# Distances on GpSimd in place of comparisons on VectorE, in the first stage of a two-layer graph-attention kernel

## The chip, the cores and the metric

One core of a Trainium2 chip runs the whole program. The metric is the device time of one execution in microseconds (us); lower is better. The median of three runs of the kernel before is 651.15 us (650.93 to 651.38). A difference of 0.2%, 1.3 us, is about what a measurement of this kernel can tell from none.

## The reference

The kernel computes two graph-attention layers on 512 nodes with 768 features, then a residual and a layer norm. There are 16896 edges (`src`, `dst`), sorted by `dst`.

```
def gat_layer(x, W, a_s, a_d, b, edge_index, concat):
    h = (x @ W).reshape(n, H, C)              # H = 8 heads of 768, then 1 head of 768
    alpha_s = einsum('nhc,hc->nh', h, a_s)
    alpha_d = einsum('nhc,hc->nh', h, a_d)
    e = leaky_relu(alpha_s[src] + alpha_d[dst], 0.2)
    e = exp(e - segment_max(e, dst)[dst])
    alpha = e / (segment_sum(e, dst)[dst] + 1e-16)
    return segment_sum(h[src] * alpha[:, :, None], dst) + b

h = elu(gat_layer(x, W1, a_src1, a_dst1, b1, ...))
out = layernorm(x + gat_layer(h, W2, a_src2, a_dst2, b2, ...))
```

The kernel replaces the edge list by a dense 512 x 512 table `cnt` (how often node s is a source of node d) and works with dense attention from there on. Building that table is the part that the change touches.

## The kernel before

**The stages.** The first stage, some 62 us, builds `cnt` and at the same time computes the first head's features `HS[0] = x @ W1[0]`. After it comes a loop over the 8 heads (attention, aggregation, the second layer's matmul, the next head's features), and at the end the second layer's attention and the layer norm. The loop and the end are the same in both kernels.

**Counting.** The edges lie as 132 chunks of 128 edges, one edge per partition. For a chunk `c`, a count is a matmul of two tables that are made from the indices:

- `os`, 128 x 512: which of the 512 nodes is the edge's source. `one_hot` (L512) makes it on VectorE by a comparison (`is_equal`, L517) or, for the 128 destinations of group `S = 2`, on ScalarE as a step function (`Sign`, L515), which `counted_by_steps` (L399) turns back into counts by a difference of neighbours. `os` tiles come from a ring of 32 buffers.
- `od` (profile name `odw`), 128 x 210 x 32: which of 32 neighbouring destination nodes is the edge's destination. Since the edges are sorted, each chunk can only hit one or two blocks of 32 nodes; there are 210 (chunk, block) pairs. `destinations(lo, hi)` (L491) makes a quarter of `od` in one VectorE instruction (L493), 128 x 1632 or 128 x 1728 elements: `rel` (destination minus the block's base) compared with 0 to 31.

`count` (L532) issues the matmuls of a batch (L543); a matmul takes the 32 columns of `od` as weights, and four blocks of 32 rows go side by side. When all of a group's blocks are done, ScalarE and VectorE move the group from PSUM into `cnt` and `absent`.

**The order** of everything is written out by hand (a manual schedule): what the Python program emits first, an engine runs first. The loop over `batches` (L575) has nine rounds. A round emits: the quarter of `od` if one of its chunks is the first of a new quarter (quarter 0 in round 0, quarter 2 in round 1, quarter 1 in round 3, quarter 3 in round 5); `sources`, the VectorE `os` of the round, with the pending `empty` steps of matmul results in the middle; `extra` steps such as `weight_sums`, the Strassen-like sums of `x` (`s1` to `s4`) or logits; then some products of the first projection, `items[pos]`, each followed by its `empty` (a ScalarE copy `hs`, L426, or a VectorE add, L428) and by some ScalarE `os` of the next round (`ahead`, `share` of them per product); then `count`.

- The products come in the order P1, P2, P5, P3, P6, P7, P4, two halves each, six matmul instructions of 128x384 per half (L305). They go through PSUM buffers `held` (2) and `mm` (3).
- `turn_x(t, r)` (L200) transposes a piece of `x` on TensorE into an `mm` buffer, and ScalarE copies it to `xT` (L205). Pieces (0,1), (1,1) follow product 1, pieces (2,0), (3,0), (2,1), (3,1) follow product 3.
- `found` and `pst` (L614) add up the edges that lie in their blocks; if not all do, a general pass follows. With these inputs it does not.

**The weights.** The sums of W1 that the products need are partly made by accumulating DMAs on GpSimd's queue: `additions0[0]` (L160) adds W1 parts into `t2` (for P6), L381 into the part for P7, `additions0[1]` (L161) from `t2` into `t4` (for P4). GpSimd writes such a DMA's descriptors itself. `load_w1(1)` and its sums (L106, L117, L160, L161 again) follow on the same queue. `weight_sums` emits all of them. The DMAs from SyncE's and ScalarE's queues count on a ring of eight semaphores, so a DMA is issued only when the eighth one before it has landed.

Of the kernel before, what the change touches and what calls it, by code (L numbers as in the profile page):

```python
# [8 lines left out]
F32 = mybir.dt.float32  # L9
F16 = mybir.dt.float16  # L10
BF16 = mybir.dt.bfloat16
I32 = mybir.dt.int32
U16 = mybir.dt.uint16
AF = mybir.ActivationFunctionType
ALU = mybir.AluOpType
# [21 lines left out]
def gat_pass(  # L37
# [16 lines left out]
    nc = tc.nc  # L54
    P = 128
    N, D = x.shape
    H = a_src1.shape[0]
    E = src.shape[0]
    NT = N // P
    DC = D // P  # L60
    HALF = D // 2
    EC = E // P
    EH = EC // 2
    HK = DC // 2
    HN = N // 2
    L, R = slice(0, HALF), slice(HALF, D)
# [10 lines left out]
    ohp = counting.enter_context(tc.tile_pool(name="onehot", bufs=1))  # L77
# [20 lines left out]
    W1, W2, A = {}, {}, {}  # L98
# [22 lines left out]
    def load_w1(h, slot="w2"):  # L121
        return load_w(W1, h, slot, w1[:, h * D:(h + 1) * D])
# [15 lines left out]
    def block(m, r, cols):  # L138
        return m[r * HK * P:(r + 1) * HK * P, cols].rearrange("(k p) d -> p k d", p=P)

    w1_0 = w1[:, :D]
    for r, cols in enumerate((L, R)):
        nc.scalar.dma_start(x_sb[:, :2, cols], x[:2 * P, cols].rearrange("(t p) d -> p t d", p=P))
        nc.sync.dma_start(W1[0][r][:, :, L], block(w1_0, r, L))
    for t in (2, 3):
        nc.sync.dma_start(x_sb[:, t, :], x[t * P:(t + 1) * P, :])
    b1_rows = ohp.tile([H * DC, P], F32, name="b1_rows")
# [5 lines left out]
    def sums_by_dma(W_, m, slot):  # L153

        lo_, hi_, t1_ = W_
        t2, t4 = (wpool.tile([P, HK, HALF], F32, name=f"{slot}t{j}") for j in (2, 4))
        for t_, cols in ((t2, R), (t4, L)):
            nc.sync.dma_start(t_, block(m, 1, cols))

        additions = [lambda: nc.gpsimd.dma_start(t2, t1_, accum_op=ALU.add),  # L160
                     lambda: nc.gpsimd.dma_start(t4, t2, accum_op=ALU.add)]  # L161
        return dict(P1=lo_[:, :, L], P2=hi_[:, :, L], P3=hi_[:, :, R], P4=t4, P5=t1_, P6=t2,
                    P7=lo_[:, :, R]), additions
# [16 lines left out]
    nodes = ohp.tile([P, N], F16, name="nodes")  # L180
# [6 lines left out]
    ones = const.tile([P, 1], F32, name="ones")  # L187
# [3 lines left out]
    for j in range(2):  # L191
        nc.vector.tensor_reduce(picks[:, j:j + 1], ident.rearrange("p (j k) -> p k j", k=32)[:, j, :], axis=AX.X,
                                op=ALU.add)
# [6 lines left out]
    def turn_x(t, r):  # L200

        ps = mm.tile([P, 512], F32, name="mm")
        for k in range(HK):
            nc.tensor.transpose(ps[:, k * P:(k + 1) * P], x_sb[:, t, (r * HK + k) * P:(r * HK + k + 1) * P], ident)
        nc.scalar.copy(xT[:, r * HK:(r + 1) * HK, t * P:(t + 1) * P],  # L205
                       ps[:, :HALF].rearrange("p (k n) -> p k n", n=P))
# [4 lines left out]
    if general:  # L211
        nc.vector.tensor_copy(idx_f, idx_i)
        idx = ohp.tile([P, 2, EC], F32, name="idx")
# [6 lines left out]
    else:  # L220
# [3 lines left out]
        B, SLACK = 32, 10  # L224
        blocks = []
        for c in range(EC):
            m = (c + 0.5) * P * N / E
            b = int(m // B)
            lo, hi = b - (m - b * B < SLACK), b + ((b + 1) * B - m < SLACK)
            blocks.append(range(max(lo, 0), min(hi, N // B - 1) + 1))  # L230
        at = [0]
        for b in blocks:
            at.append(at[-1] + len(b))
        NB = at[EC]
# [5 lines left out]
        lo = 0  # L240
        while lo < EC:
            hi, k = lo + 1, len(blocks[lo])
# [7 lines left out]
            lo = hi  # L250
# [9 lines left out]
        rel = ohp.tile([P, NB], F16, name="rel")  # L260
        nc.vector.tensor_tensor(rel, psi[:, :NB], base, op=ALU.subtract)
        idx = ohp.tile([P, EC], F32, name="idx")
# [55 lines left out]
    def logits(h, feats, t):  # L318
        for al, a, sign in zip(AL[h], A[h], (1.0, -1.0)):
            nc.vector.scalar_tensor_tensor(scr, feats[:, t, :], sign, a, op0=ALU.mult,  # L320
                                           op1=ALU.mult, accum_out=al[:, t:t + 1])
# [52 lines left out]
        ]  # L374
        return [pair(p, i, *rest) for p, *rest in steps for i in range(2)]

    def weight_sums():

        nc.vector.tensor_tensor(W1[0][2], W1[0][0][:, :, L], W1[0][0][:, :, R], op=ALU.add)
        additions0[0]()  # L380
        nc.gpsimd.dma_start(W1[0][0][:, :, R], block(w1_0, 1, R), accum_op=ALU.add)  # L381
        additions0[1]()
        load_w1(1, "w2")()
        B_, additions1 = sums_by_dma(W1[1], w1[:, D:2 * D], "w2")
        for f in additions1:
            f()
        return B_
# [67 lines left out]
    def leak(q):  # L455
        nc.vector.scalar_tensor_tensor(q, q, NEG_SLOPE, q, op0=ALU.mult, op1=ALU.min)
# [18 lines left out]
    if not general:  # L475


        S = 2
# [9 lines left out]
        cps, done = {}, set()  # L488
        od = ohp.tile([P, NB, B], BF16, name="odw", bufs=1)

        def destinations(lo, hi):  # L491
            lo, hi = at[lo], at[hi]
            nc.vector.tensor_tensor(od[:, lo:hi, :],  # L493
                                    rel[:, lo:hi].unsqueeze(2).to_broadcast([P, hi - lo, B]),
                                    nodes[:, :B].unsqueeze(1).to_broadcast([P, hi - lo, B]),
                                    op=ALU.is_equal)

        def inside():

# [2 lines left out]
            nc.vector.scalar_tensor_tensor(below, rel, 0.0, below, op0=ALU.is_ge, op1=ALU.mult, accum_out=found)  # L502

        nidx = ohp.tile([P, EC], F32, name="nidx")
        nc.scalar.activation(nidx, idx, AF.Copy, bias=0.5, scale=-1.0)

        def by_steps(b):
            return b * B // P == S
# [1 line left out]
        hot = {}  # L510

        def one_hot(c, steps):  # L512
            hot[c, steps] = o = ohp.tile([P, N], BF16, name="os", bufs=32)
            if steps:
                nc.scalar.activation(o, nodes, AF.Sign, bias=nidx[:, c:c + 1])  # L515
            else:
                nc.vector.tensor_scalar(o, nodes, idx[:, c:c + 1], None, op0=ALU.is_equal)  # L517
# [40 lines left out]
        s1, s2, s3, s4 = xsums  # L558

        def ask():  # L560
            nc.vector.tensor_scalar(flag, pst[:1, :1], -1.0, float(E), op0=ALU.mult, op1=ALU.add)

        extra = {0: [inside], 1: [lambda: B1.update(weight_sums()), ask, s1, s2, s4], 3: [s3],
                 5: [lambda: logits(0, HS[0], 0)],
                 6: [lambda: logits(0, HS[0], 1), lambda: logits(0, HS[0], 2)], 7: [lambda: logits(0, HS[0], 3)]}
        B1 = {}
        wants = [3, 4, 7, 10, 12, 14, 16, 18]
        batches = []
        for ours, theirs in ((16, 0), (8, 8), (8, 8), (12, 4), (12, 4), (12, 4), (13, 3), (14, 2), (4, 0)):
            take = [order[k][:m] for k, m in ((False, ours), (True, theirs))]  # L570
            del order[False][:ours], order[True][:theirs]
            batches.append(take[0][:ours // 2] + take[1] + take[0][ours // 2:])
        assert not any(order.values())
        pos, made, quarter, waiting = 0, set(), EC // NT, []
        for n, batch in enumerate(batches):  # L575
            for k in sorted({c // quarter for c in batch} - made):
                destinations(k * quarter, (k + 1) * quarter)
                made.add(k)
            sources(kinds(batch, False), waiting)
            ahead = kinds(batches[n + 1], True) if n + 1 < len(batches) else []  # L580
            items_here = max(wants[n] - pos if n < len(wants) else 0, 1)
            share = -(-len(ahead) // items_here)
            waiting = []
            for f in extra.pop(n, []):
                f()
            while n < len(wants) and pos < wants[n]:
                if pos == wholes:
                    pairs = projection(1, XA, B1)
                    items += [(m, e, False) for m, e in pairs[:4]]
                multiply, empty, on_vector = items[pos]  # L590
                multiply()
                if on_vector:
                    waiting.append(empty)
                else:
                    empty()
                pos += 1
                for t, r in turns.get(pos, []):
                    turn_x(t, r)
                for c in ahead[:share]:
                    one_hot(c, True)  # L600
                del ahead[:share]
            assert not ahead
            if n == 2:
                turn_b1()
            if n + 1 == len(batches):
                spread(0)
                q = [lift(0, t) for t in range(NT)]
                for t in range(NT - 1):
                    leak(q[t])
                for t in range(NT - 1):  # L610
                    rank(q[t], t)
            if n == 0:
                pst = mm.tile([P, 512], F32, name="mm")
                nc.tensor.matmul(pst[:1, :1], found, ones, start=True, stop=True)  # L614
            if n == 3:
                again = nc.values_load(flag[:1, :1], min_val=0, max_val=E)
            count(batch, n + 1 == len(batches))
        assert not extra and not waiting and pos == len(items) and len(done) == NT
    else:
        for t in range(NT):  # L620
            ps = mm.tile([P, 512], F32, name="mm")
            for c in range(EC):
                o1 = ohp.tile([P, P], BF16, name="od", bufs=4)
                o2 = ohp.tile([P, N], BF16, name="os", bufs=32)
                nc.vector.tensor_scalar(o1, nodes[:, t * P:(t + 1) * P], idx[:, 0, c:c + 1], None,
                                        op0=ALU.is_equal)
                nc.vector.tensor_scalar(o2, nodes, idx[:, 1, c:c + 1], None, op0=ALU.is_equal)
                nc.tensor.matmul(ps[:, :N], o1, o2, start=c == 0, stop=c == EC - 1)
            counted(t, ps)
            for r in range(2):  # L630
                turn_x(t, r)
        turn_b1()
        B1 = weight_sums()
# [449 lines left out]
```

## Time and profile before

| what | value |
|---|---|
| median of three runs | 651.15 us |
| the profiled execution's own time | 651.15 us |
| its span, first to last instruction | 649.4 us |
| around the span (launch, end) | 1.75 us |
| busy: PE / DVE / ACT / POOL | 637.7 / 520.4 / 276.7 / 47.2 us |
| granted TensorE clock | 0.998 |

All times in the text below are us from the span's start in the profiled execution. PE is TensorE's matmuls, PEld its weight loads, DVE is VectorE, ACT is ScalarE, POOL is GpSimd, SP is SyncE. A line such as `L517 DVE TENSOR_SCALAR os<-nodes,idx` names the line of the kernel, the engine, the operation, and the tiles written and read. The chain is the run of work that ended last, followed back from the last instruction to what released each step. A timeline line holds the start, the length, the engine, and in square brackets how long the engine was idle before it and what ended that.

### The profile page before, as it was taken

To read this page: it belongs to the slowest core of one execution; us is meant where nothing else is said; L and a number is where in the kernel's file an instruction comes from. 1 tells how busy PE (TensorE), PEld (TensorE's weight loads), DVE (VectorE), ACT (ScalarE), POOL (GpSimd) and SP (SyncE) were. 2 spreads that over 40 slices of the span, in tenths; PEclk is the share of its full clock that TensorE was granted. 3 is DMA by queue.
4 is the path that set the end of the run, shared out by engine and by line. 5 is a ranking of instruction groups with operands and counts; after the bars stand their busy time and mean duration, and the time that the engine had idled before them with its cause. 6 is when DMAs were issued, how large, how long until landed. Compare 5 with 4: busy or idle time off the path is not lost.

```text
span 649.4 us, 7212 instructions
## 1 busy us (share of the span) xinstructions
PE 637.7 (98%) x2383; PEld 404.2 (62%) x2383; DVE 520.4 (80%) x1141; ACT 276.7 (43%) x481; POOL 47.2 (7%) x90
## 2 busy tenths in 40 slices
PE   8999999999999999999999999999999999999995
PEld 4544586557755586557755586557755586645553
DVE  8989989978779777878779777878779777876875
ACT  6774744530736045430736045430736045243440
POOL 1310020011000010011000110011000010000000
PEclk9999999999999999999999999999999999999999
DMA  9993499196806792196705793196706892000122
GB/s 320 327 202 86 79 330 287 36 260 207 196 0 164 161 275 97 37 262 201 197 1 144 180 276 97 37 264 204 193 1 167 207 250 97 25 1 1 32 58 78
DMA packets 77644, 97.97 MB, mean 151 GB/s; under 512 B 37095, under 2 KB 60447, under 8 KB 77599
## 3 DMA queue, kind: packets, MB, share of 16 engines
q1 hardware_dynamic: 63934, 75.80, 37.0%
q0 software_dynamic: 12976, 20.65, 18.3%
q10 hardware_dynamic: 688, 0.98, 0.5%
q8 instruction: 21, 0.34, 0.2%
q14 instruction: 25, 0.20, 0.1%
HBM read 85.09 MB, written 1.57 MB: 133 GB/s over the span
## 4 chain that ended last, share of the span: by engine, by line
PE 96%; ACT 1%; DMA 1%; DVE 1%; issue 0%; SPq 0%
PE mm L305 64%; PE mm L764 20%; PE mm L710 3%; PE mm L1035 3%; PE held L305 2%; PE tr L543 1%; DMA w<-in_L_gnn_W_dram 1%; ACT os L515 1%; PE bc L446 0%; PE bc L543 0%; PE tr L963 0%; PE tr L679 0%; ACT xT L205 0%; DVE os L517 0%; PE bc L985 0%
## 5 line engine op out<-in xcount | busy, mean ns | idle before, releaser
L305 PE MATMUL mm<-w,gT 128*128 128x384 f32 x288 | 97.4, 487 | 0.0
L305 PE MATMUL mm<-w,xT 128*128 128x384 f32 x264 | 88.4, 488 | 0.0
L305 PEld LDWEIGHTS mm<-w,gT 128*128 128x128 f32 x288 | 53.9, 190 | 35.3 <-issue 1.6
L305 PEld LDWEIGHTS mm<-w,xT 128*128 128x128 f32 x264 | 49.8, 190 | 35.7 <-ACT os L515 0.8
L768 ACT COPY u<-mm 128x256 f32<-128x256 f32 x21 | 7.8, 372 | 142.0 <-PE mm L764 142.0
L463 ACT ACTIVATE q<-q,nmax 128x512 f32<-128x512 f32 x36 | 25.8, 721 | 89.8 <-DVE nmax L461 89.8
L764 PE MATMUL mm<-PT,hs 128*128 128x256 f32 x252 | 61.3, 379 | 0.0
L305 PE MATMUL mm<-w1t,gS 128*128 128x384 f32 x180 | 60.7, 486 | 0.0
L305 PE MATMUL mm<-w2t,xS 128*128 128x384 f32 x168 | 56.6, 487 | 0.0
L764 PEld LDWEIGHTS mm<-PT,hs 128*128 128x128 f32 x252 | 47.8, 190 | 8.4 <-issue 0.4
L363 DVE TENSOR_TENSOR h<-h,mm 128x384 f32<-128x384 f32 x72 | 39.6, 550 | 14.6 <-PE mm L305 14.0
L305 PEld LDWEIGHTS mm<-w1t,gS 128*128 128x128 f32 x180 | 34.1, 190 | 23.6
L305 PEld LDWEIGHTS mm<-w2t,xS 128*128 128x128 f32 x168 | 31.8, 190 | 22.4 <-ACT q L452 0.4
L687 ACT COPY nr<-q 128x1024 uint16<-128x1024 uint16 x32 | 33.4, 1043 | 23.3 <-DVE q L673 15.8
L764 PE MATMUL mm<-pS,gS 128*128 128x256 f32 x168 | 43.2, 380 | 0.0
L692 ACT COPY PT<-zr 128x1024 uint16<-128x1024 uint16 x32 | 37.1, 1160 | 2.0 <-DMA zr<-nr 2.0
L764 PEld LDWEIGHTS mm<-pS,gS 128*128 128x128 f32 x168 | 31.8, 190 | 4.7 <-DVE pS L737 0.4
L305 PE MATMUL mm<-w,gS 128*128 128x384 f32 x96 | 32.6, 486 | 0.0
L305 PE MATMUL mm<-w1t,gT 128*128 128x384 f32 x96 | 32.5, 487 | 0.0
L305 PE MATMUL mm<-w,xS 128*128 128x384 f32 x96 | 32.5, 487 | 0.0
L106 POOL DMA_DIRECT2D w1t<-in_L_gnn_W_dram x7 | 8.9, 1267 | 310.7 <-PE mm L305 96.5
L363 DVE TENSOR_TENSOR u<-u,mm 128x384 f32<-128x384 f32 x28 | 15.4, 552 | 19.0 <-PE mm L305 18.7
(187 smaller groups left out, 1083.3 us busy)
## 6 DMA issues: line engine op xcount, KB each, us to landing
w<-in_L_gnn_W_dram SPq DMA_DIRECT2D x90, 384.0 KB, 6.3
w<-in_L_gnn_W_dram POOLq DMA_DIRECT2D x16, 576.0 KB, 9.7
w2t<-in_L_gnn_W_dram SPq DMA_DIRECT2D x10, 576.0 KB, 4.9
w1t<-in_L_gnn_W_dram SPq DMA_DIRECT2D x9, 576.0 KB, 4.6
w2t<-in_L_gnn_W_dram POOLq DMA_DIRECT2D x8, 576.0 KB, 9.8
w1t<-in_L_gnn_W_dram POOLq DMA_DIRECT2D x7, 576.0 KB, 8.7
a_s<-in_L_gnn_a_src_dram SPq DMA_DIRECT2D x8, 384.0 KB, 3.8
a_d<-in_L_gnn_a_dst_dram SPq DMA_DIRECT2D x8, 384.0 KB, 4.2
```

What stands on the lines that cost most here:

```text
L106: nc.gpsimd.dma_start(t1, upper[:, :, R], accum_op=ALU.add)
L305: nc.tensor.matmul(ps[:, :HALF], A_[p][:, k, i * P:(i + 1) * P], B_[p][:, k, :], start=start and k == 0, stop=k == HK - 1, skip_group_chec ...
L363: nc.vector.tensor_tensor(a, a, ps, op=ALU.subtract if p == "P7" else ALU.add)
L463: nc.scalar.activation(q, q, AF.Exp, bias=nmax, scale=-1.0)
L515: nc.scalar.activation(o, nodes, AF.Sign, bias=nidx[:, c:c + 1])
L543: nc.tensor.matmul(cps[t][r:r + B, :N], od[:, at[c] + b - blocks[c][0], :], h_, start=todo[b] == hits[b], stop=todo[b] == 1, tile_position ...
L687: nc.scalar.copy(apart.rearrange("p (h n) -> p h n", h=2), q.bitcast(U16).rearrange("p (n h) -> p h n", h=2))
L692: nc.scalar.copy(PT.rearrange("p s n -> p (s n)").bitcast(U16).rearrange("p (s n h) -> p s n h", s=NT, h=2)[:, :, t * P:(t + 1) * P, :], p ...
L710: nc.tensor.matmul(ps[:, :N], HS[h][:, s, c * P:(c + 1) * P], PT[:, s, :], start=(s == 0), stop=(s == NT - 1))
L764: nc.tensor.matmul(bank[p][:, :HN], A_[p][:, k, c * P:(c + 1) * P], B_[p][:, k, :], start=over is None and k == 0, stop=k == 1, skip_group ...
L768: nc.scalar.copy(u, part("P1"))
L1035: nc.tensor.matmul(ps[:, :cols.stop - cols.start], PT[:, s, t * P:(t + 1) * P], h2[:, s, cols], start=(s == 2), stop=(s == 1))
```

## The change

Four things are changed, all in the first stage.

1. Quarter 0 of `od` is still made by VectorE's comparison. The other three quarters are made in three instructions each: GpSimd subtracts (`rel` minus 0..31, into a float32 tile `dist`), GpSimd multiplies `dist` by itself, and ScalarE takes `Relu(1 - dist)`, which is 1 at distance 0 and 0 elsewhere. The GpSimd work of quarters 2 and 1 is emitted at the start, behind the `base` memsets and ahead of the first accumulating DMA; that of quarter 3 inside `weight_sums`, behind L381 and ahead of `additions0[1]`. `dist` has two buffers. The ScalarE step of quarter 2 is emitted after product 2, those of quarters 1 and 3 at the ends of rounds 2 and 4.
2. The first part of W1 (128 x 3 x 384) is loaded by three DMAs in place of one, so two more DMAs are in the ring of semaphores.
3. The step `nidx` moves behind product 1 and its transposes, the first round's ScalarE `os` are dealt two per product in place of three, and the batches change: group S gets 5, 5, 3, 0 chunks in rounds 4 to 7 where it had 4, 4, 3, 2, so its count is complete one round earlier.
4. The `os` ring shrinks from 32 to 30 buffers.

The core of the diff:

```diff
-        nc.sync.dma_start(W1[0][r][:, :, L], block(w1_0, r, L))
+        for ks in (slice(0, 1), slice(1, 2), slice(2, HK)) if r == 0 else (slice(0, HK),):
+            nc.sync.dma_start(W1[0][r][:, ks, L], block(w1_0, r, L)[:, ks])
...
     nc.gpsimd.dma_start(W1[0][0][:, :, R], block(w1_0, 1, R), accum_op=ALU.add)
+    if between:
+        between()
     additions0[1]()
...
-        def destinations(lo, hi):
-            lo, hi = at[lo], at[hi]
-            nc.vector.tensor_tensor(od[:, lo:hi, :],
-                                    rel[:, lo:hi].unsqueeze(2).to_broadcast([P, hi - lo, B]),
-                                    nodes[:, :B].unsqueeze(1).to_broadcast([P, hi - lo, B]),
-                                    op=ALU.is_equal)
+        def distances(out, lo, hi, engine, op):
+            engine.tensor_tensor(out, rel[:, lo:hi].unsqueeze(2).to_broadcast([P, hi - lo, B]),
+                                 nodes[:, :B].unsqueeze(1).to_broadcast([P, hi - lo, B]), op=op)
+        def destinations(k):
+            lo, hi = at[k * EC // NT], at[(k + 1) * EC // NT]
+            if k == 0:
+                distances(od[:, lo:hi, :], lo, hi, nc.vector, ALU.is_equal)
+                return
+            d = ohp.tile([P, -(-NB // NT) + 2, B], F32, name="dist", bufs=2)[:, :hi - lo, :]
+            distances(d, lo, hi, nc.gpsimd, ALU.subtract)
+            nc.gpsimd.tensor_tensor(d, d, d, op=ALU.mult)
+            return lambda: nc.scalar.activation(od[:, lo:hi, :], d, AF.Relu, bias=ones, scale=-1.0)
...
-            hot[c, steps] = o = ohp.tile([P, N], BF16, name="os", bufs=32)
+            hot[c, steps] = o = ohp.tile([P, N], BF16, name="os", bufs=30)
...
-        extra = {0: [inside], 1: [lambda: B1.update(weight_sums()), ask, s1, s2, s4], 3: [s3],
+        extra = {0: [inside], 1: [lambda: B1.update(weight_sums(lambda: rest.update({3: destinations(3)}))), ask, s1, s2, s4], 3: [s3],
...
-        for ours, theirs in ((16, 0), (8, 8), (8, 8), (12, 4), (12, 4), (12, 4), (13, 3), (14, 2), (4, 0)):
+        for ours, theirs in ((16, 0), (8, 8), (8, 8), (12, 4), (12, 5), (12, 5), (13, 3), (14, 0), (4, 0)):
...
+        destinations(0)
+        rest = {S: destinations(S), 1: destinations(1)}
+        relu = {2: 1, 4: 3}
         for n, batch in enumerate(batches):
-            for k in sorted({c // quarter for c in batch} - made):
-                destinations(k * quarter, (k + 1) * quarter)
-                made.add(k)
...
-            share = -(-len(ahead) // items_here)
+            share = len(ahead) // (items_here + 1) if n == 0 else -(-len(ahead) // items_here)
...
+                if pos == 2:
+                    rest.pop(S)()
+                if pos == 1:
+                    nc.scalar.activation(nidx, idx, AF.Copy, bias=0.5, scale=-1.0)
                 for c in ahead[:share]:
                     one_hot(c, True)
                 del ahead[:share]
-            assert not ahead
+            for c in ahead:
+                one_hot(c, True)
+            if n in relu:
+                rest.pop(relu[n])()
```

## The prediction

> **What bounds the kernel now.** I read the page's chain first: TensorE carries it.
>
> ```profile
> PE 96%; ACT 1%; DMA 1%; DVE 1%; issue 0%; SPq 0%
> ```
>
> The change only touches the first 62 us, so next the windows (columns: length, then busy time of PE, PEld, DVE, ACT, POOL, with instruction counts; last the clock, DMA share, GB/s):
>
> ```profile
> 6.90:13.60 6.70, 6.24 (x24) 3.96 (x25) 6.67 (x22) 4.34 (x10) 0.00 (x0) 1.00 1.06 379
> 13.60:41.85 28.25, 27.50 (x190) 14.33 (x188) 26.19 (x64) 20.93 (x40) 6.31 (x5) 1.00 1.08 305
> 41.85:62.50 20.65, 19.48 (x138) 9.52 (x132) 19.86 (x60) 11.63 (x22) 2.54 (x2) 1.00 0.50 107
> ```
>
> VectorE is as full as TensorE: 32.86 of 34.95 us up to 41.85, with GpSimd almost free. Taking VectorE work away looks right. But TensorE is busy too: what can be won are its gaps, which the chain in order of time shows (start, length, what):
>
> ```profile
> 9.57 0.48 ACT hs L426
> 10.05 0.76 ACT xT L205 x2
> 10.82 1.84 ACT os L515 x3
> 12.65 0.37 ACT hs L426
> 13.02 1.84 ACT os L515 x3
> ...
> 41.59 0.19 DVE os L517
> ...
> 41.85 0.56 DVE hs L428
> ...
> 59.43 0.60 ACT steps L403
> ...
> 60.12 0.69 DVE cnt L405
> 60.81 1.06 DVE os L517 x4
> ```
>
> From 9.57 to 16.4 ScalarE sets the time, at 41.5 and 59.4 a late VectorE does. The decisive view is the timeline, where GpSimd and VectorE write at once:
>
> ```profile
> 1.85 1.72 POOL L249 MEMSET base<- 128x6 f32 x48
> 2.10 1.50 DVE L246 COPY pick<-ident 66x6 f32<-66x6 f32 x1
> ...
> 28.63 1.92 DVE L517 TENSOR_SCALAR os<-nodes,idx 128x512 bf16<-128x512 f16 x7
> 29.32 1.35 POOL L161 DMA_DIRECT2D w1t<-w1t  x1 [6.86 <-DMA w1t<-w1t]
> ...
> 42.78 0.89 POOL L160 DMA_DIRECT2D w2t<-w2t  x1 [9.51 <-DMA w2t<-in_L_gnn_W_dram]
> ...
> 46.62 3.50 DVE L517 TENSOR_SCALAR os<-nodes,idx 128x512 bf16<-128x512 f16 x13
> 48.59 1.66 POOL L161 DMA_DIRECT2D w2t<-w2t  x1 [4.92 <-DVE os L517]
> ```
>
> A `pick` copy took 1.50 us, against a median of 0.156 for this line, and ended at 3.60, when the 48 memsets of GpSimd ended (3.57). The other way round, the same kind of descriptor write took 0.89 us once, but 1.35 and 1.66 us when a run of comparisons (L517) was under way, and ended 0.12 us after that run (30.67 against 30.55, 50.25 against 50.12). So in each direction one engine stood until the other's run of instructions was through. The comparisons, most of what VectorE does here, are among the instructions that this happens to.
>
> **The change part by part.** The sums are made against the profiled execution, 651.15 us (span 649.4, 1.75 around it), which is also the median.
>
> *VectorE, removed:* quarters 2 and 1 at 1.95 us each and quarter 3 at 1.85 (L493): 5.75 us.
>
> *GpSimd, added:* six two-operand instructions, four of 1728 columns, two of 1632. The trace has none. The nearest rows:
>
> ```profile
> L181 POOL IOTA nodes<- 128x512 f16 x1 | 0.6, 552 | 0.4 <-POOLq L1069 0.4
> masks.py:199 POOL TENSOR_SCALAR_AFFINE_SELECT ident<-ident 128x128 f32<-128x128 f32 x1 | 0.3, 292 | 0.1
> ```
>
> The iota only writes: 552/512 = 1.08 ns a column, so 1.86 us for 1728. The affine select also reads: 292/128 = 2.28 ns, so 3.94 us for 1728 and 3.72 for 1632. I take the select, since the new instructions read two operands: 4 x 3.94 + 2 x 3.72 = 23.2 us. The iota's rate gives 11.0.
> The Trainium skill, GPSIMD Engine Reference, section Elementwise — side-by-side cycle accounting, gives 4497 ns for a two-input operation of 2048 columns, and advises VectorE for such work; an estimate from it is 3.79 us for 1728 columns, some 0.9 us less over the six than by the select.
>
> *ScalarE, added:* three `Relu` of 1728 or 1632 columns. Its rows go from 0.717 us at 512 columns (`os`, L515) to 1.160 at 1024 (L692), 0.87 ns a column: 1.77 us each. The first stands in the chain above. There two `os` leave (2 x 0.61) and `nidx` (0.31) comes in: with the `Relu` +0.8 us. The other two lie in ScalarE's idle time (7.3 us of 28.25 in the second window).
>
> *The first W1 part in three:* product 1 starts at 7.37, 0.8 us after its last other need, waiting for the whole part. With thirds it can start at about 6.6: -0.75, which the 0.8 on ScalarE eats. The two more issues on SyncE push its later loads back. The x rows of t = 2 would wait for the first x part (landed 4.38, by the wait of the `b_rows` issue) instead of going out at 2.58; bounds nothing to 1.8 us late, and their transposes start only at 13.9, so I take nothing.
>
> *Wait added:* product 2's `Relu` waits for GpSimd. Behind it on ScalarE are two `os` and the copies `xT`, and for those TensorE's transposes and all counting wait. By the rows, the first count matmul starts 4.65 us after quarter 2's distances are there: 1.77 for the `Relu`, 1.23 for two `os`, 1.67 from the first `xT` copy (14.74) to the matmul (16.41). `rel` is ready at 6.85. With GpSimd undisturbed the distances are there at 6.9 + 2 x 3.94 = 14.8, and the first count starts at 19.45 in place of 16.41: +3.0.
>
> *Steps dealt anew:* group S is complete a round earlier, so steps, `cnt` and the four late `os` leave the end: of the 3.1 us from 59.43 to 62.53, TensorE needs about 1.2 (four transposes and eight matmuls), so up to -1.9. The gap at 41.5 goes with VectorE's load: -0.95. Two `os` buffers fewer let VectorE run ahead 0.5 us less; covered while it is the late one, and 0.5 at most otherwise.
>
> *Sharing.* This decides. If the two engines run one after the other, VectorE's remaining 32.86 - 5.75 = 27.1 us, less six additions from PSUM (L428, 3.3 us) that may run beside GpSimd, plus GpSimd's 23.2 make 47.0 us, where 34.95 were used: +12.05 by 41.85. TensorE has no reserve there, since VectorE feeds it. With -1.9 at the end: +10.15.
> The rows are not all of one mind: at 42.78 a descriptor write came through in 0.89 us between comparisons that it merely stretched (a group maximum of 0.447 against 0.344). If that is how it goes, the pair costs a few tenths.
> The Trainium skill, SBUF — State Buffer, section Who interferes with whom, states that GpSimd and a VectorE instruction in a two-port mode, or with two SBUF operands against a reading GpSimd, exclude each other for the whole instruction; taken strictly it gives the sum above, the 42.78 row alone would give rival B.
> I take the exclusive case, because three of the four rows show it, and because each new instruction would hold what it holds for four microseconds where a descriptor write does for tenths.
>
> **The rivals.**
>
> *A, the forecast: exclusive.* +10.15, 661.3 us. Low end: only the front pays, VectorE's 6.67 and GpSimd's 7.9 one after the other from 6.9, first count at 21.5 (+5.1), gaps won (-2.85): 653.4. High end: the PSUM additions don't overlap (+3.3) and the end is not won (+1.9): 666.5.
>
> *D, exclusive, and the weight sums late as well.* The accumulating DMA L160 (issued at 20.11, 8.9 us to landing) stands behind four of the new instructions. One after the other: 6.9 + 15.8 + 6.67 + 4.6 (VectorE's work to there) = 34.0, landing 42.9, just in time for product P6 (31.23 + 12). L161 stands behind quarter 3 as well: 34.0 + 1.6 + 7.4 + 5.8 of VectorE = 48.8, landing 57.7, where P4 would start at 54.5: +3.2, up to 8 if GpSimd keeps losing the port. I put it at +5: 666.3.
>
> *B, shared without holding, at the select's price.* +3.0 at the front, -2.85 in the gaps: +0.2, 651.3 us, from 650.3 to 653. For it: the 0.89 row, and that a comparison writes only part of its time.
>
> *C, faster: shared, and GpSimd quicker than the select.* ScalarE reaches the `Relu` at about 11.8 (9.57 - 0.75 for the earlier start, then two copies of x, `nidx`, two `os`, two `hs`). If the distances are there by then, under (11.8 - 6.9)/2 = 2.45 us an instruction, nothing waits: front +0.05, gaps -2.85: 648.35 us. The iota's 1.86 would do it; the copy that stood 1.50 us speaks against it. That GpSimd doesn't really take the work is no rival: it has no other place to run.
>
> **How the numbers follow.** A 0.56, D 0.14, B 0.14, C 0.16. The time is A's, 661.3. A, D and most of B and C lie between 648.5 and 668; beyond it I leave about 0.1 below, for C's full sum, and 0.05 above. Faster by over 0.2% (under 649.85, 1.3 us, about what a measurement can tell): C, and 0.04 of B: 0.2. Within: 0.05 of B. Slower: A, D and 0.05 of B: 0.75. A and D together have their own range, 653 to 668.
>
> **What would show it.** In the changed kernel's profile: the duration of the GpSimd subtract and multiply (near 3.9 us alone; longer, or beginning beside stretched L517 comparisons, if they exclude each other); VectorE comparisons or the quarter 0 instruction of several us instead of 0.35 and 1.85; a ScalarE wait for GpSimd ahead of the first `Relu`, and the first count matmul after 21 us instead of 16.41; TensorE waits for `os`, `xS` or the DMA into `t4` up to 45 us; the end without the steps chain. I am wrong if comparisons keep 0.35 us while GpSimd runs (then B, or C under 2.45 us), or if TensorE's first stage ends before 62.5. After the first stage nothing should differ.

## The result, and the profile after

The changed kernel takes 666.67 us (median of 6 runs, 665.66 to 667.55), the kernel before 651.14 us (6 runs, 650.93 to 651.38): a ratio of 1.0239 [1.0229, 1.0249], so 15.5 us more. The profiled execution of the changed kernel took 666.95 us with a span of 665.2, that is 15.8 us more span than before; the rest of this section is about those 15.8.

The chain of the whole span still belongs to TensorE, but VectorE's share, too small for the row before, is now 6%:

```profile
PE 93%; DVE 6%; issue 0%; ACT 0%; DVEq 0%
```

The comparisons explain where that comes from. The row of groups gives busy time, mean in ns of one, and the idle time before them. There are 105 of them, as before, and before they took 29.5 us in all:

```profile
L529 DVE TENSOR_SCALAR os<-nodes,idx 128x512 bf16<-128x512 f16 x105 | 44.9, 499 | 3.7 <-PE tr L555 3.5 <-ACT os L527 0.2
```

The timeline of the front (start, length, engine, line, what; in brackets the idle time before it and its releaser) shows the mechanism. L496 is the subtraction on GpSimd and quarter 0's comparison on VectorE, L508 the square, L509 the `Relu`, L634 the matmul on `found`, L555 the counting:

```profile
7.79 3.08 POOL L496 TENSOR_TENSOR dist<-rel,nodes 128x1728 f32<-128x1728 f16 x1 [4.22 <-DVE rel L263]
7.83 4.76 DVE L496 TENSOR_TENSOR odw<-rel,nodes 128x1632 bf16<-128x1632 f16 x1
10.96 4.56 POOL L508 TENSOR_TENSOR dist<-dist 128x1728 f32<-128x1728 f32 x1
12.52 12.80 DVE L529 TENSOR_SCALAR os<-nodes,idx 128x512 bf16<-128x512 f16 x16
15.48 3.13 POOL L496 TENSOR_TENSOR dist<-rel,nodes 128x1728 f32<-128x1728 f16 x1
15.55 1.74 ACT L509 ACTIVATE odw<-dist,ones 128x1728 bf16<-128x1728 f32 x1 [2.96 <-POOL dist L508]
18.69 3.07 POOL L508 TENSOR_TENSOR dist<-dist 128x1728 f32<-128x1728 f32 x1
...
26.01 0.16 PE L634 MATMUL mm<-ones,found 128*1 128x1 f32 x1 [5.54 <-DVE below L515]
...
26.06 2.72 PE L555 MATMUL tr<-os,odw 128*32 128x512 bf16 x19
```

Read it as two engines that pass one thing to and fro. The subtraction ends at 10.87; quarter 0 on VectorE began at almost the same moment and needs 1.85 us (its time before), but is done only at 12.59: it stood 2.9 us. The square is issued at 10.96 and is done at 15.52; the next instruction of the same length takes 3.07, so it stood until 12.5, when quarter 0 was through. Then the 16 comparisons of the first batch: the first three take 3.15, 3.17 and 3.22 us, each beside one GpSimd instruction, the other thirteen 0.335 each. The train takes 12.80 us where it took 4.28. `found`, which TensorE waits for ahead of the first count, is made behind that train.

The second place is quarter 3's pair:

```profile
33.04 7.62 DVE L529 TENSOR_SCALAR os<-nodes,idx 128x512 bf16<-128x512 f16 x4
34.06 3.47 POOL L496 TENSOR_TENSOR dist<-rel,nodes 128x1632 f32<-128x1632 f16 x1
37.61 2.91 POOL L508 TENSOR_TENSOR dist<-dist 128x1632 f32<-128x1632 f32 x1
...
41.18 0.26 PE L472 MATMUL mm<-ident,b_rows 48*128 48x48 f32 x1 [1.92 <-DVE hs L432]
```

Four comparisons in 7.62 us, where four took 1.13 before; TensorE waits for the addition `hs` that stands behind them. The third of the four takes 4.12 us: it began at 33.57, while GpSimd wrote the descriptors of L383 (33.28, 1.29 us), and ended at 37.69, after the subtraction. The fourth, beside the square, takes 3.05.

The windows (length; busy time of PE, PEld, DVE, ACT, POOL; the granted clock) show what TensorE's standstill brings with it: from 15 to 25 it is busy for 1.55 of 10 us, and its granted clock goes to half and stays there after work has come back.

```profile
15.00:20.00 5.00, 1.08 (x5) 1.08 (x6) 5.00 (x3) 3.83 (x6) 4.92 (x3) 0.70 1.06 387
20.00:25.00 5.00, 0.47 (x3) 0.07 (x1) 5.00 (x14) 3.27 (x6) 1.75 (x1) 0.50 1.03 399
25.00:30.00 5.00, 3.99 (x26) 1.71 (x27) 4.97 (x17) 2.46 (x4) 0.00 (x0) 0.50 0.90 322
```

The end of the stage still has its steps and its late comparisons:

```profile
70.72 0.69 DVE L409 TENSOR_TENSOR cnt<-steps 128x512 f32<-128x512 f32 x1 [0.63 <-ACT steps L408]
71.33 3.76 DVE L529 TENSOR_SCALAR os<-nodes,idx 128x512 bf16<-128x512 f16 x14
...
76.89 1.13 DVE L529 TENSOR_SCALAR os<-nodes,idx 128x512 bf16<-128x512 f16 x4
...
77.29 1.39 PE L555 MATMUL tr<-os,odw 128*32 128x512 bf16 x8 [0.94 <-DVE os L529]
```

By stations of TensorE's work, the changed kernel is late by 9.65 us at the first count (26.06 against 16.41), 11.8 at P5 (33.19 against 21.38), 14.6 at P3's second half (43.78 against 29.20), 15.6 at P4 (58.08 against 42.45) and 16.2 at the first product behind the stage's last count (78.61 against 62.46). Behind the stage it loses nothing more.

VectorE's own sum comes near the 14.6 at P3. Beside GpSimd it lost 4.76 - 1.85 = 2.9 us in quarter 0, 12.80 - 4.28 = 8.5 in the first train and 7.62 - 1.13 = 6.5 at quarter 3: 17.9. It was given back quarters 2 and 1, 3.9 by then, and started 0.9 later (`rel` was ready at 7.7 against 6.85). 17.9 - 3.9 + 0.9 = 14.9.

### The profile page after: what moved, and what is told of

Its sections match the earlier page's. It is cut to its first block, busy times and chain, and to the rows that moved or that the text cites. A ratio compares the mean times of both kernels' runs of the same rounds, so it can differ in the third digit from the quotient of the medians.

```text
span 665.2 us, 7220 instructions
## 1 busy us (share of the span) xinstructions
PE 641.9 (97%) x2383; PEld 407.2 (61%) x2383; DVE 533.5 (80%) x1138; ACT 282.0 (42%) x484; POOL 65.7 (10%) x96
## 4 chain that ended last, share of the span: by engine, by line
PE 93%; DVE 6%; issue 0%; ACT 0%; DVEq 0%
PE mm L307 61%; PE mm L784 19%; DVE os L529 4%; PE mm L730 3%; PE mm L1055 3%; PE held L307 2%; PE tr L555 1%; DVE odw L496 1%; PE bc L179 1%; PE bc L450 0%; PE bc L555 0%; PE tr L983 0%; DVE scr L322 0%; PE tr L699 0%; PE mm L206 0%
## 5 line engine op out<-in xcount | busy, mean ns | idle before, releaser
L365 DVE TENSOR_TENSOR h<-h,mm 128x384 f32<-128x384 f32 x72 | 39.7, 551 | 14.6 <-PE mm L307 14.0
L529 DVE TENSOR_SCALAR os<-nodes,idx 128x512 bf16<-128x512 f16 x105 | 44.9, 499 | 3.7 <-PE tr L555 3.5
L707 ACT COPY nr<-q 128x1024 uint16<-128x1024 uint16 x32 | 33.4, 1044 | 23.3 <-DVE q L693 16.2
```

The source lines that it names most:

```text
L365: nc.vector.tensor_tensor(a, a, ps, op=ALU.subtract if p == "P7" else ALU.add)
L707: nc.scalar.copy(apart.rearrange("p (h n) -> p h n", h=2), q.bitcast(U16).rearrange("p (n h) -> p h n", h=2))
```

## The experiments

The theory was that the two engines exclude each other, instruction against instruction, and that VectorE's lost time sets the stage. The rivals: the `Relu` and its wait on ScalarE, the clock, the new dealing and smaller ring, and a sharing of which only the place mattered. Each comparison is with the runs of the kernel before on the same chip (median 651.04 to 651.14).

**All destinations back on VectorE; the rest of the change stays** (5 rounds)

```diff
 def destinations(k):
     lo, hi = at[k * EC // NT], at[(k + 1) * EC // NT]
+    distances(od[:, lo:hi, :], lo, hi, nc.vector, ALU.is_equal)
-    if k == 0:
-        distances(od[:, lo:hi, :], lo, hi, nc.vector, ALU.is_equal)
-        return
...
-rest = {S: destinations(S), 1: destinations(1)}
-relu = {2: 1, 4: 3}
...
+for k in sorted({c // quarter for c in batch} - made):
+    destinations(k)
+    made.add(k)
```

> The changed kernel with all four quarters of the destinations back on VectorE's comparison, each made where the kernel before made it; the load in three, the new dealing of steps and the ring of 30 stay. Theory 1 (GpSimd and VectorE exclude each other): with no GpSimd arithmetic the loss of 15.5 us goes whole, 648.5 to 652 us; the gap of 3.1 us at the end of the stage may shrink. Theory 2 (ScalarE's Relu waits for slow GpSimd, and the copies behind it hold TensorE): the same. Theory 3 (the new dealing or the load cost part of the 15.5 us): over 653 us.

652.0 us, ratio 1.0014 [1.0005, 1.0023]. The whole loss but 0.9 us goes with GpSimd's work, and what remains of the change gains nothing: its last count begins no earlier than before, and TensorE waits 1.1 us for an `hs` addition and 0.9 for the last comparisons.

**The kernel before, with the load in three alone** (5 rounds)

```diff
-nc.sync.dma_start(W1[0][r][:, :, L], block(w1_0, r, L))
+for ks in (slice(0, 1), slice(1, 2), slice(2, HK)) if r == 0 else (slice(0, HK),):
+    nc.sync.dma_start(W1[0][r][:, ks, L], block(w1_0, r, L)[:, ks])
```

> The kernel before with nothing but the first W1 part loaded in three. Product 1 started at 7.37 for want of that part and could start at 6.6; the copies on ScalarE behind it set the time up to 16.4. If the third that it waits for is the limit: -0.75, 650.4 us. If the transposes ahead of it or the clock are the limit, as in the profile of the changed kernel (product 1 at 7.28, the full clock only from 6.75): 651.1. Slower only if the later loads come late: over 651.7.

650.78 us, ratio 0.9998 [0.9989, 1.0007]: not to be told from before. Its profile has product 1 at 6.29 instead of 7.37 and a span 0.9 shorter, but the moment at which the granted clock becomes full also differs from one execution to the next (4.97 before, 4.71 here, 6.75 in the changed kernel), so one profile can't show what this part is worth.

**The kernel before, with the six GpSimd instructions and nobody who reads them** (3 rounds)

```diff
+def distances(lo, hi):
+    lo, hi = at[lo], at[hi]
+    d = ohp.tile([P, -(-NB // NT) + 2, B], F32, name="dist", bufs=2)[:, :hi - lo, :]
+    nc.gpsimd.tensor_tensor(d, rel[:, lo:hi].unsqueeze(2).to_broadcast([P, hi - lo, B]),
+                            nodes[:, :B].unsqueeze(1).to_broadcast([P, hi - lo, B]), op=ALU.subtract)
+    nc.gpsimd.tensor_tensor(d, d, d, op=ALU.mult)
...
+distances(S * quarter, (S + 1) * quarter)
+distances(quarter, 2 * quarter)
...
+weight_sums(lambda: distances(3 * EC // NT, EC))
```

> The kernel before, VectorE making all destinations, with the six GpSimd instructions of the change added at the same places of GpSimd's queue and the ring of 30; nobody reads what they write, and there is no Relu. Theory 1 (exclusion): VectorE loses up to the 18.3 us that GpSimd works (six times 3.05), less what falls into idle time: 660 to 669 us, with comparisons and the quarter 0 instruction of 3 us and more. Theory 2 (the wait of the Relu): nobody waits, 651 to 652 us. Theory 3 (late accumulating DMAs behind the GpSimd work): 652 to 656 us, with TensorE waiting for a DMA.

667.8 us, ratio 1.0245 [1.0230, 1.0261]. No `Relu` is there, nothing waits for GpSimd's results, and the loss is all there, a little more of it since VectorE keeps its destinations too. The timeline has the same picture line by line:

```profile
7.98 4.77 DVE L495 TENSOR_TENSOR odw<-rel,nodes 128x1632 bf16<-128x1632 f16 x1
...
12.67 12.80 DVE L526 TENSOR_SCALAR os<-nodes,idx 128x512 bf16<-128x512 f16 x16
```

So the wait of product 2's `Relu`, 2.96 us in the changed kernel, is real and decides nothing.

**The changed kernel, with 48 matmuls on zeros in TensorE's two standstills** (3 rounds)

```diff
-for t, r in turns.get(pos, []):
+for j, (t, r) in enumerate(turns.get(pos, [])):
+    if pos == 3 and j == 2:
+        keep_warm(22)
     turn_x(t, r)
+if pos == 3:
+    keep_warm(26)
```

> The changed kernel with 22 and 26 matmuls of zeros put into TensorE's two standstills (ahead of the third transpose after product 3, and ahead of the first count). In the changed kernel the granted clock was 0.5 from 17.0 to 30.65 us, and the first count with half a product took 5.7 us where it took 3.5. If idling brings the clock down: it stays at 1.0, 664.5 us (-2.2). If the clock came down for another reason: 666.7. The exclusion stays in any case: the first count still starts at about 26 us.

668.05 us, ratio 1.0254 [1.0238, 1.0270]: no gain. The clock now stays full up to 39 us, the first counts and product 2's second half go at full speed, and P5 starts at 30.34 instead of 33.19 (0.9 of it from an earlier start of this execution: product 1 at 6.41 instead of 7.28). But VectorE's standstill at quarter 3 has not moved with it:

```profile
32.19 7.60 DVE L529 TENSOR_SCALAR os<-nodes,idx 128x512 bf16<-128x512 f16 x4
...
40.31 0.34 PE L472 MATMUL mm<-ident,b_rows 48*128 48x48 f32 x1 [3.90 <-DVE hs L432]
```

TensorE waits 3.9 us there instead of 1.9, and P3's second half starts at 43.69, against 43.78 without those matmuls. TensorE stood idle again there (busy for 1.41 of the 4 us from 35 to 39), and the clock now fell to half from 39.0 to 45.9: counting took 3.4 us from 40.31 to P3's second half, where it took 2.6 at full clock in the changed kernel, and that half product 3.29 instead of 2.20. So the half clock was not removed but moved, and that is why this kernel ends no earlier. What the run does show is that the clock follows TensorE's standstill, and that up to 40.3 the full clock gains nothing: the wait for `hs` ends 0.87 us earlier than in the changed kernel (40.31 against 41.18), as much as this execution started earlier, because VectorE sets the time there.

**The changed kernel without the square** (3 rounds)

```diff
-nc.gpsimd.tensor_tensor(d, d, d, op=ALU.mult)
```

> The changed kernel without the multiplication: the Relu then gets distances that are not squared, so the counting matrices are other ones; GpSimd has three instructions left of six, some 9.7 us (3.08 + 3.13 + 3.47) of 18.3. Theory 1 (what GpSimd holds VectorE for is what is lost): at the front one of the three comparisons of 3.1 us or two of them go back to 0.33, so the first count starts 3 to 5.6 us before 26.06; quarter 3 holds VectorE for one instruction in place of two, some 2.8 less. Loss 15.5 - 5.6 - 2.8 = 7.1, so about 658, and 656 if the half clock does not come either. Rival (the loss is fixed by the new order: Relu's wait, steps dealt anew, clock): it stays above 12, so 663 or more.

658.85 us, ratio 1.0114 [1.0099, 1.0130]. The first count starts at 20.4, 5.7 us earlier than in the changed kernel. With three GpSimd instructions the time is 6.85 us above the first experiment's 652.0, with six 14.7: half the instructions, about half the loss. That is no fixed price for each, as the next run shows.

**The changed kernel with quarter 3 alone on GpSimd** (3 rounds)

```diff
-if k == 0:
+if k != 3:
     distances(od[:, lo:hi, :], lo, hi, nc.vector, ALU.is_equal)
...
```

> The changed kernel with only quarter 3 by GpSimd and ScalarE; quarters 0, 2 and 1 by VectorE where the kernel before has them. Nothing of the front is touched, the first count should start at 16 us. Theory 1: the two GpSimd instructions hold VectorE for about 6.5 us, in which it gets some 4 comparisons done, and it is given back 1.85: 3 to 4 us net, of which 2.8 reached TensorE in the changed kernel; with 0.9 of the new dealing 654.8 (653 to 656). Rival (all of the loss comes from the front; late in the stage VectorE has room for it): 652.0, as with all destinations on VectorE, or a few tenths better for the 1.85 us given back.

659.36 us, ratio 1.0124 [1.0109, 1.0140]: dearer than both expected. The front is undisturbed (first count at 16.09), so VectorE now stands elsewhere in its program when quarter 3's instructions start, at the sums for which the next product waits:

```profile
21.77 5.50 DVE L288 TENSOR_TENSOR xS<-xS,xT 128x768 f32<-128x768 f32 x1
...
22.67 3.78 POOL L496 TENSOR_TENSOR dist<-rel,nodes 128x1632 f32<-128x1632 f16 x1
...
26.52 3.51 POOL L508 TENSOR_TENSOR dist<-dist 128x1632 f32<-128x1632 f32 x1
27.31 3.54 DVE L290 TENSOR_TENSOR xS<-xT,xS 128x768 f32<-128x768 f32 x1
...
30.95 3.86 PE L307 MATMUL mm<-w,xS 128*128 128x384 f32 x6 [5.02 <-issue]
```

The two sums take 0.96 us each in the changed kernel; here 5.50 and 3.54, so VectorE lost 7.1. Of that TensorE lost 5.15 at once: P3 starts at 30.95, in the first experiment at 25.80. Its standstill then brought the half clock once more (the window from 30 to 35; the granted clock is the third number from the end):

```profile
30.00:35.00 5.00, 4.05 (x11) 2.01 (x15) 5.00 (x12) 0.15 (x1) 3.56 (x4) 0.66 1.14 279
```

P3's first half took 3.86 us instead of 2.10, 1.76 more, and the lateness against the first experiment stays at 6.9 to the end of the stage. With the 0.9 of that experiment this is 7.8, measured 8.3. So two GpSimd instructions cost 7.4 us here, where three cost 6.85 without the square: what a pair costs hangs on which VectorE work it meets. A pair that cost 2.8 at P3 when TensorE was already late costs much more when it is not.

**The changed kernel with its first 16 comparisons in another form** (3 rounds)

```diff
+elif len(hot) <= 16:
+    nc.vector.tensor_scalar(o, nodes, idx[:, c:c + 1], 0.0, op0=ALU.is_equal, op1=ALU.add,
+                            accum_out=sums[:, len(hot) - 1:len(hot)])
 else:
     nc.vector.tensor_scalar(o, nodes, idx[:, c:c + 1], None, op0=ALU.is_equal)
```

> The changed kernel with the first 16 comparisons of VectorE written so that each also gives its sum (an accumulator nobody reads); same result otherwise. Theory 1, that it is the form of the instruction that makes the two engines exclude each other: these comparisons keep one duration (0.35 to 0.7 us) although GpSimd works beside them, the train of 16 takes 5.6 to 11.2 us in place of 12.8, and the first count starts at 20.2 (set by the Relu) to 24.5 in place of 26.06: 661 to 665. The Trainium skill, SBUF - State Buffer, section Who interferes with whom, says that the form that also writes out its accumulator does not enter the modes that take the shared port. Rival (whatever VectorE reads or writes beside GpSimd stands): three comparisons still take 3.1 us, and 16 accumulator reads of 0.075 us come on top: 667 to 668.

The instruction's length is the answer:

```profile
12.49 0.73 DVE L530 TENSOR_SCALAR_CACHE_REDUCE os<-nodes,idx 128x512 bf16<-128x512 f16 x1
...
15.46 3.07 POOL L496 TENSOR_TENSOR dist<-rel,nodes 128x1728 f32<-128x1728 f16 x1
...
22.50 0.73 DVE L530 TENSOR_SCALAR_CACHE_REDUCE os<-nodes,idx 128x512 bf16<-128x512 f16 x1
```

All sixteen take 0.73 us, one every 0.667, beside GpSimd (to 21.68) and after it. Same operands, same engine, same neighbour: it is the form of the VectorE instruction that makes it stand. The Trainium skill, SBUF — State Buffer, section Who interferes with whom, leaves the form that also writes out its accumulator out of those that can contend, and tells of an exclusive hold for the whole instruction in the two-port modes; these runs agree, with 0.73 us for the one form and 3.15 to 3.22 for the other, though no trace shows the mode itself. As a remedy it is worth little: 16 times 0.667 is 10.7 us against 12.8, and against 4.28 without GpSimd. The first count in the profile comes at 23.95 instead of 26.06, but quarter 3's pair (TensorE waits 2.7 us for `hs`) and a second stretch at half clock (40.9 to 44.3) take most of that back: 0.5 us are left at the end of the stage. The time, 664.8 us, is inconclusive: the four runs lie at 662.5, 662.9, 666.8 and 666.9, and the profile is of an execution of 666.75 us; what went otherwise in the two shorter ones is open.

**What the rest of the change is worth without GpSimd.** Three kernels. The first is the kernel before with the load in three (as in the second experiment) and 40 `os` buffers instead of 32:

```diff
-hot[c, steps] = o = ohp.tile([P, N], BF16, name="os", bufs=32)
+hot[c, steps] = o = ohp.tile([P, N], BF16, name="os", bufs=40)
```

> The kernel before with its first W1 part loaded in three and 40 os buffers in place of 32: what could be had of the change's aims without GpSimd. Theory 1 (VectorE is late because it waits for free buffers: 0.73 us at 41.32, with TensorE's gaps of 0.42 at 36.82 and 0.95 at 41.5 behind it): 0.5 to 1 us faster than before, 650.1 to 650.6. Rival (VectorE is late by its own work, and a larger ring lets it do nothing more): as with the load in three alone, 650.8, which can't be told from before.

650.4 us, ratio 0.9987 [0.9978, 0.9996]. The second is the first experiment's kernel, new dealing and all, with 40 buffers instead of 30:

```diff
-hot[c, steps] = o = ohp.tile([P, N], BF16, name="os", bufs=30)
+hot[c, steps] = o = ohp.tile([P, N], BF16, name="os", bufs=40)
```

> The changed kernel with all destinations back on VectorE and 40 os buffers in place of 30: the load in three and the steps dealt anew alone, without the smaller ring. Theory 1 (the ring of 30 cost what the new dealing gained): VectorE's wait of 1.8 us for TensorE's counting goes, TensorE's waits of 0.9 and 1.1 us at the end of the stage too, and the time falls from 652.0 to 649 to 650. Rival (the dealing itself gains nothing, since cnt, the logits and the last comparisons stand behind each other on VectorE at the end in this order too): 651.0 to 652.0.

650.85 us, ratio 0.9997 [0.9988, 1.0006], against 1.0014 with a ring of 30: TensorE's 1.1 us wait for `hs` ahead of P4 is gone, its 0.9 us for the last comparisons is still there. So the smaller ring is probably what cost the 0.9 (the two intervals overlap only at their edges), and the new dealing gains nothing. The third takes the end differently: the first of the three, with VectorE's last four comparisons issued ahead of `cnt`.

```diff
...
+            if n + 2 == len(batches):
+                sources(kinds(batches[n + 1], False), waiting)
+                waiting = []
             count(batch, n + 1 == len(batches))
```

> The kernel before with its first W1 part loaded in three, 40 os buffers, and VectorE's last four comparisons issued ahead of cnt, where VectorE stands idle for 0.8 us (59.36 to 60.16). Theory 1 (TensorE's last wait, 0.74 us for those comparisons, and their 1.1 us behind cnt are on the path): last product of the stage 1 to 1.2 us earlier than 62.5, cnt and the absences 0.3 later, time 649.2 to 649.7. Rival (ScalarE's and VectorE's work on the first softmax sets the time there, which cnt now reaches later): 650.4 to 650.7.

650.28 us, ratio 0.9986 [0.9977, 0.9995]: no better than the first. The first product behind the stage does start 1.9 us earlier, at 60.56 instead of 62.50 (0.8 of it from an earlier start of this execution), and then TensorE waits in the next stage, where the kernel before and the other two have no wait at all:

```profile
82.09 1.13 PE L770 MATMUL mm<-pS,gS 128*128 128x256 f32 x4 [0.94 <-DVE pS L743]
```

The first and the third of these are the fastest kernels of the study, by 0.13 and 0.14%. Their intervals lie wholly below 1, but that is less than the 0.2% which the prediction took as measurable, and no more is claimed.

## Why the prediction was right, and where its sum was not

*Case A was the case.* The engines exclude each other, VectorE's stage pays, slower: forecast 661.3 us, range 648.5 to 668.0, measured 666.67. This is inside the range, but 0.2 above the upper end of what A by itself was given (653.4 to 666.5). Adding the same GpSimd work to the kernel before gives the loss by itself, half of the instructions give about half of it, and the accumulator form shows that VectorE's standing hangs on the form of its instruction. The direction and the mechanism were right; that 661.3 came within 5.4 us is in part luck, since two errors of the sum pull against each other. With GpSimd's six instructions at their measured price (next paragraph) the same sum would have given +5.2 us, 656.3, a third of the 15.5 measured.

*GpSimd's instruction, 3.94 us, was too dear.* It takes 3.07 to 3.13 for 1728 columns, 1.78 ns a column, and the six together, without the time that they stood themselves, some 18.2 us instead of 23.2. The select's 2.28 ns a column was the nearer row of the two, but still over a quarter too high. The Trainium skill's figure (GPSIMD Engine Reference, section Elementwise — side-by-side cycle accounting), from which 3.79 was estimated, is nearly a quarter too high for these instructions as well.

*The sum came out too low because the credits against it were not there.* The sum gave A's 23.2 back 3.3 for additions that read PSUM, 5.75 of VectorE's relief, 2.1 of VectorE's idle time and 1.9 at the end. VectorE in fact lost 17.9 us beside GpSimd, about all that GpSimd worked. GpSimd's instructions fell beside quarter 0 and comparisons, not beside the additions. Of the relief only 3.9 came before P3; the last 1.85 fell where VectorE then waited 3.55 us for free `os` buffers. And the idle time was of no use: it lay at 34.1 and 40.6 in the profile before (1.26 and 0.73 us), behind the places at which GpSimd now worked.

*The gaps (-0.95 and -1.9).* This is the term that was wrong in kind. The gap at 41.5 became a wait of 1.1 us, with the ring of 30 as its probable cause. At the end `cnt` did move ahead by a round, but the four late comparisons did not: they now stand behind fourteen others and the logits, and TensorE waits 0.94 us for them, 0.74 before. Even where TensorE's late start there was removed, most of it came back as a wait for VectorE in the next stage. 1.9 us of idle time on a chain was counted as 1.9 us of gain without asking what comes second.

*The front.* A's low end had the first count at 21.5, from VectorE's and GpSimd's work one after the other up to the first square. It left out that quarter 1's two instructions follow at once and take two more turns from the same train, and that `found`, behind the train, is ahead of the first count on TensorE. It came at 26.06. The half clock was not forecast either; it costs 2 us at P5, which VectorE's lateness at quarter 3 covers.

*Smaller terms.* The `Relu` was to take 1.77 us and takes 1.74. The load in three was to gain 0.75, eaten by ScalarE's 0.8; alone it gains nothing that can be measured. The two x rows behind it brought no wait.

*The rivals.* D gave 666.3, nearest to the result, by a mechanism that did not occur: the accumulating DMA was issued at 30.55 and P6 started at 45.8, and TensorE has no wait for a DMA in the stage. A number that fits is no evidence for its case. B and C are out for these instructions; what B describes, comparisons that keep their time beside GpSimd, exists in the accumulator form. The row that spoke for B, a descriptor write between comparisons that were merely stretched, was a poor model for two arithmetic instructions of 3 us.

## What to carry to other kernels

Before work is moved to an idle GpSimd, look at which forms the VectorE instructions beside it have: comparisons with a per-partition scalar and two-operand SBUF instructions stood for as long as GpSimd worked (0.335 us became 3.15, 1.85 became 4.76, 0.96 became 5.50), so the "idle" engine's time was VectorE's time, some 18 us for a relief of 5.75. Price such a move as GpSimd's full length on VectorE, at the place where VectorE will then be, and start from no credit for overlap; then ask what the chain's engine loses there, which was 2.8 us at one place and 6.9 at another for the same pair. A gap on the critical chain is a gain only down to the next-latest chain; find that one in the stage behind before the gap is entered in a sum.

## What the runs showed of the hardware that was not expected

The hold passes to and fro by single instructions. The prediction read the rows of before as one engine standing until the other's whole run was through; in fact, of a train of sixteen comparisons and three waiting GpSimd instructions, one comparison went with each GpSimd instruction, 3.15 to 3.22 us long, and the other thirteen followed when GpSimd was done.

The granted clock fell to 0.5 while TensorE was nearly idle (busy for 1.55 us from 15 to 25), and was still 0.5 in the window from 25 to 30, in which TensorE was busy for 3.99 of 5 us. The counting and half a product in that stretch took 5.7 us instead of 3.5.
